# Graph attention with residual and layer norm: four steps of the loop moved between iterations, seventeen tiles of rows fetched one by one, 8.1 instead of 8.25 pick blocks an iteration

## The chip, the cores and the metric

The kernel runs on one core of one Trainium2 chip. The metric is the device time of one execution in microseconds (us), from its start to its end on the chip; times shown as "median" are over several runs. A core has five engines that run side by side: TensorE (PE in the profile, its weight loads PEld), VectorE (DVE), ScalarE (ACT), GpSimd (POOL) and SyncE (SP), which only issues transfers.

## What is computed

There are 6250 nodes with 64 features and 206,250 edges, sorted by destination. Each edge has 64 features of its own. With H = 4 heads of D = 16:

```python
Qh = (x @ Wq.T + bq).reshape(n, H, D)
Kh = (x @ Wk.T + bk).reshape(n, H, D)
Vh = (x @ Wv.T + bv).reshape(n, H, D)
Ee = (edge_attr @ We.T + be).reshape(-1, H, D)
score = (Kh[src] * Qh[dst] * (1.0 / np.sqrt(D)) * Ee).sum(-1)
score = jnp.exp(jnp.clip(score, -5.0, 5.0))
msg = Vh[src] * score[..., None]
wV = jax.ops.segment_sum(msg, dst, num_segments=n)
out = layernorm(x + wV.reshape(n, H * D))
```

The sources are random, so the rows of k and v have to be fetched by index for each edge. The destinations are sorted, so queries and sums lie in narrow windows of nodes.

## The kernel before

A tile is 128 edges; there are 1612 tiles. A group (the loop's `g`) is eight tiles, 202 groups; two groups make a step, and the sums over destinations are made once a step. A prologue of some 100 us makes tables in DRAM: `kv_tab` with a row of k and v (512 bytes) for each node, `q3_tab` with q in three bf16 parts. Then one long loop, written out by hand, goes over the groups. The order of the instructions on each engine is the order of the program; engines wait for each other through semaphores. A PSUM tile's bank is used by one instruction after another: two users of one bank wait for each other in program order even where they touch different columns. The tile `room` has two banks. Both hold edge values (`ee`); the first also holds the sums (`pa`, `sum_`) and the second the weights. The tile `qe` has a bank for each of two groups; `qq` is one bank.

For group g the steps are, with the engine and the profile's line:

- `edges(g)`, PE, L691 `room<-et,we_sb`: eight f32 matmuls make the edge values, transposed (features by edges), from the loaded `et`.
- `biased(g)`, ACT, L706 `eb<-room,be_col`: adds the bias.
- `queries(g)`, PE, L691 `qq<-to,qw`: two matmuls of a window of q with one-hot rows. The one-hot rows are made on ACT by `onehot_rows` (L247) and `onehot_rows_rest` (L253) from loaded keys `kb`.
- `terms(g)`, DVE, L721 `term<-eb,qq`: product of the two.
- `turn(g)`, PE, L727 `qe<-ident,term`: four transposes, back to edges by features.
- `products(g)`, DVE, L745 and L748: product with k, and the sum over each head.
- `weigh(g)`, ACT, L754 and L756: clip and exponential; the weights lie in `room`.
- `message(g)`, DVE, L768 `qe<-room,kv`: weights times v, into `qe`.
- `keep(g, 0)`, `take(g, 0)`, `keep(g, 1)`, `take(g, 1)`, ACT L782 and DVE L787: split the message into three bf16 parts (`msg`); keep rounds, take subtracts.
- `sums(s)`, PE, L691 `room<-msg,of`: 16 matmuls a step with a one-hot of destinations (`onehot_edges`, DVE, L737), into `room`.
- `add(s)`, DVE, L822 and L828: adds a step's sums to the node rows. It runs in the odd iterations, the sums in the even ones.

The rows of k and v come in three ways. The first five groups are computed in the prologue. Most tiles are gathered by GpSimd, one indirect transfer of 128 rows a tile (`gather`, L264). The others are "picked" on PE: `hots` (DVE, L651) makes a one-hot block of sources, and `picks` multiplies it with the node features `parts`, three matmuls of 128 by 512 a block (L691 `pick<-hot,parts`). 25 blocks pick the sources' features for one set of four tiles; `picked` (DVE, L673), `picked_kv` (PE, L691 `pick<-w,x`, with `bkv_p`) and `place_kv` (ACT, L686) make k and v of them. How many blocks an iteration does is set by `first_unit`, now 33/4 = 8.25; 63 sets are made in all.

In iteration g the order before is:

- PE: edges(g+3); the set's `picked_kv`, where one is due; all picks; turn(g+1); queries(g+2); in even iterations sums.
- DVE: products(g); hots; message(g); hots; take(g,0); in odd iterations add; where due, picked; in odd iterations onehot_edges; take(g,1); terms(g+2); normalising of finished rows.
- ACT: weigh(g); biased(g+3); onehot_rows(g+4); keep(g,0); where due, place_kv; onehot_rows_rest(g+4); keep(g,1).
- SP: transfers of `et` (every second iteration), source rows, `qw` and `kb` (every second), in this order.
- POOL: the gathers for four steps on, each tied to a PE instruction (`where`, `behind`) so that they are spread over the iteration.

Of the kernel before, what the change touches and what calls it, by code (L numbers as in the profile page):

```python
# [8 lines left out]
F32 = mybir.dt.float32  # L9
BF16 = mybir.dt.bfloat16  # L10
I32 = mybir.dt.int32
U8 = mybir.dt.uint8
# [4 lines left out]
P = 128  # L17
# [38 lines left out]
def tiles_of(g):  # L56
    return min(G, T - g * G)
# [19 lines left out]
def first_unit(g):  # L77

    return (g - LEAD) * 33 // 4


def when(k):

    return max(g for g in range(LEAD + 4 * k // 33 + 2) if first_unit(g) <= k)
# [17 lines left out]
def is_picked(g, j):  # L102

    return g in ALL_PICKED and j >= tiles_of(g) - 2

# [25 lines left out]
def tile_gnn(ctx: ExitStack, tc: tile.TileContext, x, x_blocks, by_rows, xT, wT, bias, beT, weT, eT, src, src_rows, dst,  # L131
             dst_rows, out):
# [10 lines left out]
    key_tab = dram.tile([NR2, 2 * G * P], U8, name="key_tab")  # L143
    kv_v = kv_tab.rearrange("(p b) c -> p b c", p=P)
# [4 lines left out]
    kvs = [consts.tile([P, 2 * G, 2 * C], F32, name=f"kv{i}") for i in range(KVB)]  # L149

# [117 lines left out]
    def lots(s):  # L268

        some = []  # L270
        for g in groups_of(s):
            js = [j for j in range(tiles_of(g)) if not is_picked(g, j)]
            some += [(g, js[:len(js) // 2]), (g, js[len(js) // 2:])]
        return some
# [17 lines left out]
    with tc.tile_pool(name="nodes", bufs=1) as nodes, \  # L292
# [161 lines left out]
        def rest_of_q():  # L454
            q, two = late.pop(0)
            nc.scalar.activation(q3[:, two, 1], q, AF.Copy)
            nc.vector.tensor_sub(q3[:, two, 2], q, q3[:, two, 1])

        for i in range(NB // CB):
            bs = slice(i * CB, (i + 1) * CB)  # L460
            kv_sb = chunks.tile([P, CB, 2 * C], F32, name="kv_sb")
            for b in range(0, CB, 2):
# [34 lines left out]
                if place == (4, 4):  # L497
                    masks()
                pair = (i * CB + b) // 2
# [14 lines left out]
            if i == 2:  # L514
                nc.sync.dma_start(x_nodes[1], by_rows[:, 30 * C:])
                nc.sync.dma_start(dst_i[:, :KEYS], dst[:, :KEYS])
        rest_of_q()
# [84 lines left out]
    with tc.If(rv == 0) as branch:  # L602

        with tc.tile_pool(name="work", bufs=2) as work, \
# [78 lines left out]
            def place_kv(m):  # L683
                for i, g in enumerate(PICKED[m]):
                    n = tiles_of(g)
                    nc.scalar.activation(kv_of(g)[:, n - 2:n, :], rooms_of(m)[:, 2 * i:2 * i + 2], AF.Copy)  # L686

# [186 lines left out]
            for g in range(2):  # L874
                edges(g)
                biased(g)
                queries(g)
                terms(g)
            turn(0)
            edges(2)  # L880
            biased(2)
            for mc in pieces(0):
                hots(*mc)
            for g in range(NG + 1):
# [37 lines left out]
                if parted:  # L922
                    take(g, 0)
# [20 lines left out]
                if parted:  # L944
                    keep(g, 1)
# [210 lines left out]
```

## Time and profile before

| | |
|---|---|
| median of 3 runs | 2070.77 us (2070.09 to 2071.17) |
| the profiled execution | 2091.55 us, of which the span of its instructions is 2089.7 |
| clock granted to TensorE, mean | 0.946 |
| busy: PE, DVE, POOL, ACT | 82%, 75%, 62%, 48% |
| memory traffic | 97 GB/s |

The profile is of one execution, and that one is some 21 us longer than the median of the runs. Busy times are shares of the span. A row of the groups reads: line, engine, operation, output tile and input tiles, shape, count, then busy time in us and the mean of one in ns, then the engine's idle time just before these instructions and what ended most of it. In a timeline row the first two numbers are start and duration in us, and the bracket gives the idle time before it and its releaser.

### The profile page before, as it was taken

What the parts mean: (1) busy time and instruction counts of PE and PEld (TensorE: products, weight loads), DVE (VectorE), ACT (ScalarE), POOL (GpSimd) and SP (SyncE); (2) the same over time, 40 slices, a digit from 0 to 9 for tenths busy, and PEclk for the clock granted to TensorE, in tenths of its full rate; (3) what the DMA queues carried; (4) which work ended last, traced back from release to release, by engine and by line L of the source; (5) the groups of instructions that cost most, each with busy time, mean ns of one, the idle gap of its engine ahead of it and who ended that gap; (6) DMA issues with size and microseconds to landing.
All of it is one profiled execution on the core that took longest, in us unless ns stands there. A gap on an engine that the chain in (4) does not pass through costs nothing.

```text
span 2089.7 us, 29080 instructions
## 1 busy us (share of the span) xinstructions
PE 1715.4 (82%) x9720; PEld 881.7 (42%) x9907; DVE 1563.1 (75%) x2484; ACT 995.5 (48%) x1712; POOL 1287.9 (62%) x1370
## 2 busy tenths in 40 slices
PE   6488798888888888888878888888888888878864
PEld 6244344444444444444434444444444443444432
DVE  5377777777777787777777778777877777778775
ACT  3454454445444455445444454444444544445553
POOL 6566666666666666666666666666666666666552
PEclk9789999999999999999999999999999999999975
DMA  6534333333333333333333333333333333333320
GB/s 174 191 92 117 89 99 100 84 101 101 81 102 85 102 97 86 102 92 102 100 82 100 96 93 102 83 99 102 82 111 90 98 101 82 101 87 95 95 81 24
DMA packets 115175, 203.87 MB, mean 98 GB/s; under 512 B 55427, under 2 KB 56175, under 8 KB 114901
## 3 DMA queue, kind: packets, MB, share of 16 engines
q1 hardware_dynamic: 71058, 112.94, 18.2%
q0 software_dynamic: 43520, 87.91, 16.5%
q8 instruction: 80, 1.31, 0.3%
q10 hardware_dynamic: 436, 1.04, 0.2%
q14 instruction: 81, 0.66, 0.1%
HBM read 194.18 MB, written 7.59 MB: 97 GB/s over the span
## 4 chain that ended last, share of the span: by engine, by line
PE 60%; DVE 14%; issue 11%; ACT 10%; another core or an unknown queue 2%; POOL 1%; DMA 1%; DVEq 0%; POOLq 0%; ACTq 0%; SPq 0%
PE pick L691 44%; PE room L691 12%; DVE hot L651 4%; ACT eb L706 3%; DVE qe L768 3%; DVE qe L787 2%; PE qe L727 2%; PE qq L691 1%; ACT room L756 1%; ACT to L253 1%; ACT to L247 1%; PE ps L467 1%; ACT msg L782 1%; POOL kv L264 1%
## 5 line engine op out<-in xcount | busy, mean ns | idle before, releaser
L264 POOL DMA_INDIRECT kv<-kv_tab,src_i x1320 | 1248.4, 946 | 747.1 <-issue 295.2
L691 PE MATMUL pick<-hot,parts 128*128 128x512 bf16 x4538 | 1110.1, 389 | 100.3 <-issue 88.0
L691 PEld LDWEIGHTS <-parts 128*128 128x128 bf16 x4725 | 455.2, 100 | 724.9 <-issue 270.6
L651 DVE TENSOR_TENSOR hot<-from,still 128x2560 bf16<-128x2560 bf16 (+4 forms) x411 | 469.5, 1149 | 0.0
L754 ACT ACTIVATE score<-score,five_p 128x32 f32<-128x32 f32 x202 | 64.9, 321 | 756.0 <-DVE score L748 419.8
L768 DVE SCALAR_TENSOR_TENSOR qe<-room,kv 128x512 f32<-128x512 f32 x200 | 139.9, 699 | 273.4 <-ACT eb L706 243.3
L691 PE MATMUL room<-et,we_sb 64*64 64x256 f32 (+1 forms) x1616 | 151.8, 428 | 141.3 <-DVE qe L787 33.0
L782 ACT ACTIVATE msg<-qe 128x512 bf16<-128x512 f32 x400 | 236.9, 592 | 7.0 <-DVE qe L787 4.3
L253 ACT ACTIVATE to<-to,one_p 126x1024 bf16<-126x1024 bf16 x198 | 227.3, 1148 | 0.0
L691 PE MATMUL room<-msg,of 128*128 128x192 bf16 x1592 | 159.5, 254 | 81.0 <-issue 26.9
L247 ACT ACTIVATE to<-kb,minus_row 126x1024 bf16<-126x1024 uint8 x198 | 224.8, 1135 | 0.0
L721 DVE TENSOR_TENSOR term<-eb,qq 128x512 f32<-128x512 f32 x202 | 137.1, 679 | 115.1 <-PE pick L691 35.3
L787 DVE TENSOR_TENSOR msg<-qe,msg 128x512 bf16<-128x512 f32 x200 | 137.0, 685 | 65.0 <-issue 28.0
L691 PEld LDWEIGHTS <-of 128*128 128x128 bf16 x1600 | 136.5, 101 | 107.8 <-issue 79.4
L756 ACT ACTIVATE room<-score,five_p 128x32 f32<-128x32 f32 x202 | 58.8, 291 | 232.4 <-PE pick L691 180.0
L706 ACT ACTIVATE eb<-room,be_col 128x512 f32<-128x512 f32 x202 | 138.6, 686 | 25.6 <-remote 15.9
L787 DVE TENSOR_TENSOR qe<-qe,msg 128x512 f32<-128x512 f32 x200 | 139.3, 696 | 6.9 <-ACT msg L782 3.6
L748 DVE TENSOR_REDUCE score<-prod 128x32 f32<-128x512 f32 x202 | 138.3, 684 | 7.0
L745 DVE TENSOR_TENSOR prod<-kv,qe 128x512 f32<-128x512 f32 x202 | 137.2, 679 | 5.3 <-issue 2.7
L727 PE MATMUL qe<-ident,term 128*128 128x128 f32 x806 | 126.0, 280 | 5.3 <-DVE term L721 4.9
L691 PEld LDWEIGHTS room<-et,we_sb 64*64 64x64 f32 x1616 | 49.1, 138 | 191.8 <-issue 125.9
L727 PEld LDWEIGHTS qe<-ident,term 128*128 128x128 f32 x806 | 102.7, 144 | 49.0 <-DVE term L721 9.6
(139 smaller groups left out, 972.5 us busy)
## 6 DMA issues: line engine op xcount, KB each, us to landing
et<-in_eT SPq DMA_DIRECT2D x100, 512.0 KB
kb<-key_tab SPq DMA_DIRECT2D x101, 252.0 KB
kv<-kv_tab,src_i POOLq DMA_INDIRECT x1320
srcs<-in_src_rows SPq DMA_DIRECT2D x63, 256.0 KB
qw<-q_tab SPq DMA_DIRECT2D x202, 15.8 KB
kv_tab<-kv_sb SPq DMA_DIRECT2D x4, 640.0 KB
q_tab<-q SPq DMA_DIRECT2D x5, 480.0 KB
y<-in_x_blocks SPq DMA_DIRECT2D x2, 512.0 KB
```

What stands on the lines that cost most here:

```text
L247: nc.scalar.activation(TO[g][:, :n, :], KB.pop(g)[:, :n * P].rearrange("p (j e) -> p j e", j=n), AF.Square, bias=minus_row3[:3 * W])
L253: nc.scalar.activation(TO[g][:, :n, :], TO[g][:, :n, :], AF.Relu, bias=one_p[:3 * W], scale=-1.0)
L264: return nc.gpsimd.indirect_dma_start(out=kv_of(g)[:, j, :], out_offset=None, in_=kv_tab[:, :], in_offset=bass.IndirectOffsetOnAxis(ap=src ...
L651: nc.vector.tensor_tensor(HOT[k][:, :hi - lo].rearrange("p b (a c) -> p b a c", c=2), pairs(FROM[m])[:, None].to_broadcast(shape), block2[ ...
L691: mark.append(nc.tensor.matmul(*aps, **kw))
L706: nc.scalar.activation(EB[g][:, :n].rearrange("p (i r) e -> p r i e", r=2), ee[:, :, :n // 2], AF.Identity, bias=be_col)
L727: nc.tensor.transpose(qe[g % 2][:, k:k + half + 1:half, :], TERM[g][:, k, :], ident)
L745: nc.vector.tensor_mul(prod[:, :n, :], kv_of(g)[:, :n, :C], qe[g % 2][:, :n, :])
L748: nc.vector.tensor_reduce(score, prod[:, :n, :].rearrange("p g (h d) -> p g h d", h=H), axis=AX.X, op=OP.add)
L768: nc.vector.scalar_tensor_tensor(to.rearrange("p g (h d) -> p g h d", h=H), WEIGHT.pop(g)[:, :, :, None].to_broadcast([P, n, H, D]), LEAST ...
L782: nc.scalar.activation(part, left, AF.Copy)
L787: nc.vector.tensor_sub(left if i == 0 else part_of(g, 2)[1], left, part)
```

## The change

Three things are changed.

The number of pick blocks an iteration becomes 81/10 = 8.1; with it the number of sets becomes 62, and the sets' places move.

Seventeen tiles (the first tile of groups 13, 24, ... 189) are neither gathered nor picked. Their 128 rows are fetched by SyncE with one transfer for each row: the row's byte offset is read into a register from `single_i`, and 512 bytes are copied from `kv_tab` into a tile `single`. Twelve rows are fetched in an iteration, over eleven iterations a tile; two iterations after the last, ScalarE copies the tile to its place (`place_single`).

Four steps move. In iteration g the order becomes:

- PE: `picked_kv` where due; four blocks of picks; edges(g+3); turn(g+1); queries(g+2); the other picks; in even iterations sums.
- DVE: products(g); take(g-1,1); terms(g+1); hots; message(g); hots; add; picked; onehot_edges; take(g,0); normalising.
- ACT: keep(g-1,1); weigh(g); biased(g+2); place_single; onehot_rows(g+4); keep(g,0); place_kv; onehot_rows_rest(g+4).
- SP: as before, and then the twelve rows.

The diff, without the plumbing of the new input:

```diff
 def first_unit(g):
-    return (g - LEAD) * 33 // 4
+    return (g - LEAD) * 81 // 10
...
+EACH = 12
+SPAN = -(-P // EACH)
+SINGLE = list(range(SPAN + 2, NG - 3, SPAN))
...
+            def fetch_singles(g):
+                i, lo = g // SPAN, g % SPAN * EACH
+                if i >= len(SINGLE):
+                    return
+                if lo == 0:
+                    SINGLES[i] = work.tile([P, 2 * C], F32, name="single")
+                hi = min(lo + EACH, P)
+                _, vs = nc.values_load_multi_w_load_instructions(
+                    single_i[i:i + 1, lo:hi], engines=[mybir.EngineType.SP], min_val=0,
+                    max_val=(NR - 1) * 2 * C * 4, skip_runtime_bounds_check_because="rows of the sources")
+                for p, v in zip(range(lo, hi), vs):
+                    nc.sync.dma_start(SINGLES[i][p:p + 1, :].bitcast(U8), kv_bytes[:, bass.ds(v, 2 * C * 4)])
+
+            def place_single(g):
+                if g in SINGLE:
+                    nc.scalar.activation(kv_of(g)[:, 0, :], SINGLES.pop(SINGLE.index(g)), AF.Copy)
...
+                fetch_singles(g)
+                former = before and step_of[g - 1] < WHOLE
                 fetch_blocks(g)
                 where.append(mark[-1])
-                if g + 3 < NG:
-                    edges(g + 3)
+                if former:
+                    keep(g - 1, 1)
                 if now:
                     products(g)
+                if former:
+                    take(g - 1, 1)
+                if g + 1 < NG:
+                    terms(g + 1)
+                if now:
                     weigh(g)
-                if g + 3 < NG:
-                    biased(g + 3)
+                if g + 2 < NG:
+                    biased(g + 2)
                 for mc in ahead[:1]:
                     hots(*mc)
                 if now:
                     message(g)
+                place_single(g + 1)
...
-                if parted:
-                    take(g, 0)
                 for s in done:
                     add(s)
...
-                for some in by_two(todo):
+                two = by_two(todo)
+                for some in two[:2]:
                     picks(some)
                     where.append(mark[-1])
+                if g + 3 < NG:
+                    edges(g + 3)
                 if g + 1 < NG:
                     turn(g + 1)
                 if g + 2 < NG:
                     queries(g + 2)
+                for some in two[2:]:
+                    picks(some)
+                    where.append(mark[-1])
...
-                if parted:
-                    keep(g, 1)
...
                 if parted:
-                    take(g, 1)
-                if g + 2 < NG:
-                    terms(g + 2)
+                    take(g, 0)
```

More of the change, by code (lines that the diff above doesn't have):

```diff
@@ L77, in first_unit @@
 def first_unit(g):
-    return (g - LEAD) * 33 // 4
+    return (g - LEAD) * 81 // 10
 def when(k):
-    return max(g for g in range(LEAD + 4 * k // 33 + 2) if first_unit(g) <= k)
+    return max(g for g in range(LEAD + 10 * k // 81 + 2) if first_unit(g) <= k)
 LAST = max(m for m in range(1, NG) if when(UNITS * m - 1) + 8 < NG)
@@ L104, in is_picked, with is_single @@
     return g in ALL_PICKED and j >= tiles_of(g) - 2
+EACH = 12
+SPAN = -(-P // EACH)
+SINGLE = list(range(SPAN + 2, NG - 3, SPAN))
+assert SINGLE[0] >= 10
+def is_single(g, j):
+    return g in SINGLE and j == 0
 BLOCKS = (RING, 24, 4), (24, 40, READY[0] + 4), (40, BIG + 1, READY[0] + 6)
@@ L149, in tile_gnn @@
     kvs = [consts.tile([P, 2 * G, 2 * C], F32, name=f"kv{i}") for i in range(KVB)]
+    single_i = consts.tile([len(SINGLE), P], I32, name="single_i")
     def kv_of(g):
@@ L271, in lots @@
         for g in groups_of(s):
-            js = [j for j in range(tiles_of(g)) if not is_picked(g, j)]
+            js = [j for j in range(tiles_of(g)) if not is_picked(g, j) and not is_single(g, j)]
             some += [(g, js[:len(js) // 2]), (g, js[len(js) // 2:])]
@@ L873, in tile_gnn @@
             fetch_edges(2)
[L874 to L878, printed above, removed]
+            edges(0)
+            biased(0)
+            queries(0)
+            terms(0)
             turn(0)
+            edges(1)
+            biased(1)
+            queries(1)
             edges(2)
-            biased(2)
             for mc in pieces(0):
```

9 lines of the change are left out of this document (7 added, 2 removed).

## The prediction

> **What bounds the kernel now.** I read the page first (busy shares and clock), then the groups of lines, then a table by stretches, then the timeline of three iterations.
>
> ```profile
> span 2089.7 us, 29080 instructions
> PE 1715.4 (82%) x9720; PEld 881.7 (42%) x9907; DVE 1563.1 (75%) x2484; ACT 995.5 (48%) x1712; POOL 1287.9 (62%) x1370
> ...
> L264 POOL DMA_INDIRECT kv<-kv_tab,src_i x1320 | 1248.4, 946 | 747.1 <-issue 295.2
> L691 PE MATMUL pick<-hot,parts 128*128 128x512 bf16 x4538 | 1110.1, 389 | 100.3 <-issue 88.0
> L651 DVE TENSOR_TENSOR hot<-from,still 128x2560 bf16<-128x2560 bf16 (+4 forms) x411 | 469.5, 1149 | 0.0
> L691 PE MATMUL room<-et,we_sb 64*64 64x256 f32 (+1 forms) x1616 | 151.8, 428 | 141.3 <-DVE qe L787 33.0
> L691 PE MATMUL room<-msg,of 128*128 128x192 bf16 x1592 | 159.5, 254 | 81.0 <-issue 26.9
> ```
>
> PE is the busiest engine and two thirds of its work are picks. They overlap, so one costs 1110.1 us / 4538 = 245 ns, not its mean of 389. PE is idle for 2089.7 - 1715.4 = 374 us. Of that, 141.3 us end at the edge-value matmuls, 81.0 at the sums and 100.3 at the picks; the last are almost all "issue", which no reordering of data touches. So 222 us of PE's idle time stand before the two steps whose surroundings change. That is the gain's upper end.
>
> ```profile
> 300.00:1900.00 1600.00, 1359.53 (x7835) 682.22 (x7990) 1231.56 (x1871) 772.04 (x1295) 1011.79 (x1071) 0.97 0.35 95
> 926.10:933.16 7.06, 7.01 (x38) 3.19 (x39) 6.95 (x12) 4.65 (x8) 3.95 (x5) 0.94 0.15 39
> 1004.10:1012.55 8.45, 7.28 (x39) 3.24 (x39) 6.20 (x11) 4.39 (x7) 5.59 (x7) 0.92 0.19 45
> ...
> L768 DVE SCALAR_TENSOR_TENSOR qe<-room,kv 128x512 f32<-128x512 f32 x161 | 112.6, 699 | 212.9 <-ACT eb L706 191.1 <-issue 14.0 <-ACT room L756 5.2
> ```
>
> Columns of the first three: stretch, length, busy time of PE, PEld, DVE, ACT, POOL, then clock, DMA share and GB/s. The middle 1600 us hold 161 messages, so an iteration takes 1600 / 161 = 9.94 us. The iteration from 926.10 to 933.16 needs 7.06 with PE busy for 7.01 of it; the one from 1004.10 needs 8.45, and PE stands for 1.17. VectorE's message waits 212.9 us in this window, mostly for ScalarE's eb.
>
> ```profile
> 1001.90 2.27 PE L691 MATMUL room<-msg,of 128*128 128x192 bf16 x14 [1.17 <-issue]
> ...
> 1004.10 1.13 PE L691 MATMUL room<-et,we_sb 64*64 64x256 f32 x8
> ...
> 1008.16 0.29 ACT L756 ACTIVATE room<-score,five_p 128x32 f32<-128x32 f32 x1 [2.17 <-PE pick L691]
> ...
> 1008.48 0.69 ACT L706 ACTIVATE eb<-room,be_col 128x512 f32<-128x512 f32 x1
> ...
> 1009.20 0.70 DVE L768 SCALAR_TENSOR_TENSOR qe<-room,kv 128x512 f32<-128x512 f32 x1 [2.18 <-ACT eb L706]
> ...
> 1009.81 1.21 DVE L651 TENSOR_TENSOR hot<-from,still 128x2048 bf16<-128x2048 bf16 x1
> ...
> 1010.49 0.60 PE L727 MATMUL qe<-ident,term 128*128 128x128 f32 x4
> ...
> 1010.94 0.69 DVE L787 TENSOR_TENSOR qe<-qe,msg 128x512 f32<-128x512 f32 x1
> ...
> 1011.54 0.36 DVE L822 TENSOR_REDUCE room<-room 128x64 f32<-128x192 f32 x1
> ...
> 1011.93 0.28 DVE L828 SCALAR_TENSOR_TENSOR y<-room,above,y 128x64 f32<-128x64 f32 x1
> ...
> 1012.13 0.27 DVE L828 SCALAR_TENSOR_TENSOR y<-room,below,y 128x64 f32<-128x64 f32 x1
> ...
> 1012.55 0.66 PE L691 MATMUL room<-et,we_sb 64*64 64x256 f32 x8 [1.12 <-ACT to L253]
> ```
>
> This is the present ring. The tile `room` holds the edge values, the weights and the sums, and its users go one after the other. Edge values end at 1004.10 + 1.13 = 1005.23, but ScalarE's Exp, which writes `room`, starts only at 1008.16: PE's signal comes 2.93 us late, while picks run. Then biased (eb), message, hot, subtraction and add follow, and the next edge values start at 1012.55, right after the add (1012.40), PE having stood for 1.12.
>
> **The change, part by part.** *Ring cut.* Exp of iteration g now needs the edge values made in the middle of iteration g-1, with some 12 picks (12 x 0.245 = 2.9 us) and more behind them; the late signal above is about covered. The edge values stand behind four blocks (12 picks, 2.9 us) instead of at PE's start, so the add has 2.9 us more to finish. In half of the iterations (odd ones) the add still stands in front of them. I take half of 141.3: -70 us. Bounds: -141 if every wait goes, 0 if they come back at the new place (above 0: second rival).
>
> *Subtractions.* keep(g,1) and take(g,1) go behind the next products; sums(g+1) of PE still stand half an iteration behind that. Of the 81.0 us, 26.9 are "issue" and stay as they are; of the other 54 I take 20, since the subtraction now lies closer to its reader. Bounds 0 and -54. On ScalarE, keep waits at the head of the iteration and Exp is queued behind it, but Exp waits for the products anyway. On VectorE, take and terms now lie between products and message, where message idled for 212.9 us: the work hides in that wait, and ScalarE's Exp and biased (0.29 + 0.69) in the work.
>
> *Picks.* 81/10 instead of 33/4 blocks an iteration leaves 62 sets of 25 blocks instead of 63. 25 x 3 = 75 picks x 245 ns = 18.4 us off PE; one set's matmuls of k and v:
>
> ```profile
> L691 PE MATMUL pick<-w,x 128*128 128x128 f32 x504 | 79.3, 299 | 4.5 <-issue 4.3
> L686 ACT ACTIVATE kv<-pick 128x256 f32<-128x256 f32 x126 | 41.4, 387 | 6.2 <-PE pick L691 3.9 <-PE qq L691 1.6 <-PE qe L727 0.6
> ```
>
> 8 x 79.3 / 504 = 1.3 us. Together -20 us, as PE is on the path nearly everywhere (0 if another engine is). VectorE saves 469.5 x 25 / 1575 = 7.5 us beside it. The set's 4 tiles return to gathers and 17 tiles leave them: 13 gathers fewer, 12 us, hidden, since GpSimd idles for 747.1 us.
>
> *Single rows.* 17 x 128 = 2176 transfers of one row, 12 an iteration, by SyncE. Placing a tile costs ScalarE at most the 387 ns of L686, 17 times, 7 us: ScalarE is 48% busy, so nothing; the conversions behind it start that much later and are wanted some iterations on. The one product of offsets on VectorE is at the start: below 1 us. Issuing:
>
> ```profile
> 977.46 0.25 SPq L222 DMA_DIRECT2D qw<-q_tab  x1
> 977.81 0.34 SPq L241 DMA_DIRECT2D kb<-key_tab  x1
> 978.33 0.33 SPq L222 DMA_DIRECT2D qw<-q_tab  x1
> ...
> 995.39 0.36 SPq L208 DMA_DIRECT2D et<-in_eT  x1
> ...
> 999.01 0.00 SPq L222 DMA_DIRECT2D qw<-q_tab  x1
> ...
> L216 SPq TENSOR_LOAD <-base x26: 97/707/1484, 67.6 to 1973.4; - x26
> SPq L208 <- PE pick L691: 1007.9, 62, 22.3
> ```
>
> An issue with its address registers takes 978.33 - 977.81 = 0.52 us in one round, and (999.01 - 995.39) / 5 = 0.72 us in another. 12 x 0.52 + 0.71 (registers) + 1.0 (a generous half of a two-iteration round of et, kb, qw, srcs) = 8.0 us of an iteration. SyncE now waits for over 1007.9 us, so this fits; queued behind the rows are the next qw, kb and et, which are wanted two or three iterations on. I take 0. Bounds: 0 and the third rival's price.
>
> The Trainium skill, "DMA: Bandwidth & Descriptors", section "Issuing engine by pattern", gives indirect access to GpSimd and simple loads to SyncE, which speaks against this part. The trace shows no single-row transfer, so only SyncE's issue rows bear on it, and they leave room.
>
> *Clock.* The window's 0.97 means 0.03 x 1600 = 48 us of lost clock; the iteration after the 1.17 us stall at 1001.90 had 0.92. Shorter stalls may give part of it back. I count 0 and keep 48 for the range.
>
> The Trainium skill, "TensorE: Matmul & The Clock Gate", section "Why this matters for your kernels", fears only idle gaps above about 3 us. By that rule the 48 would stay lost; the row with 0.92 after 1.17 us speaks against it.
>
> **Sum.** -70 - 20 - 20 = -110 on the profiled execution's 2091.6 us (2089.7 span and 1.9 around it): 1981.6. The median of the runs is 2070.8, 20.8 lower; taken off likewise, 1960.8, say 1960.
>
> **The rivals.** *A, the forecast:* PE's waits halve; 1960.
>
> *B, slower: a new ring through the transposes.* Now message(g) -> edge values(g+3) -> turn(g+1) -> products(g+1) -> message(g+1) closes within one iteration, where before there was an iteration of slack. Its parts:
>
> ```profile
> 1013.45 0.68 DVE L787 TENSOR_TENSOR msg<-qe,msg 128x512 bf16<-128x512 f32 x1
> 1014.05 0.67 DVE L721 TENSOR_TENSOR term<-eb,qq 128x512 f32<-128x512 f32 x1
> 1014.64 0.68 DVE L745 TENSOR_TENSOR prod<-kv,qe 128x512 f32<-128x512 f32 x1
> 1015.36 0.69 DVE L748 TENSOR_REDUCE score<-prod 128x32 f32<-128x512 f32 x1
> 1015.96 1.48 DVE L651 TENSOR_TENSOR hot<-from,still 128x2560 bf16<-128x2560 bf16 x1
> ...
> 1016.98 0.29 ACT L756 ACTIVATE room<-score,five_p 128x32 f32<-128x32 f32 x1 [0.58 <-PE pick L691]
> ...
> 926.10 1.06 PE L691 MATMUL room<-et,we_sb 64*64 64x256 f32 x8
> ...
> 928.77 0.29 ACT L756 ACTIVATE room<-score,five_p 128x32 f32<-128x32 f32 x1
> ```
>
> PE 0.66 + 0.60, VectorE 0.68 + 0.69 + 0.68 + 0.67 + 1.48 + 0.70: 6.16 us plus PE's late signal. With an add before the edge values, also 1.21 + 0.36 + 0.28 + 0.27: 8.28. Mean 7.22 plus the lag. It decides once the lag exceeds 9.94 - 7.22 = 2.7 us. The lag was 2.93 above, 1016.98 - 1013.21 = 3.77 in the next iteration, and at most 928.77 - 927.16 = 1.61 in the quick one. With the mean of the first two, 3.35, an iteration takes 10.57: 0.63 x 191 iterations with picks = +120 us; 2190. For it: those two lags. Against: they were seen with a whole iteration's picks, 8.25 x 3 or some 25, in one run behind the edge values; now transposes, queries and waits of their own follow at once, and runs of picks are half as long. I expect 1 to 2 us.
>
> *C, slower: SyncE becomes the bound.* At the second round's pace 12 x 0.72 + 0.71 + 1.8 = 11.2 us an iteration, +1.2 us x 187 iterations = +225; about 2295. At 0.52 it is 8.0 and costs nothing; it decides from (9.94 - 1.7) / 12 = 0.69 us a row. Against: the pace of 0.52 is seen where nothing was in the way.
>
> *D, the waits only change place.* VectorE (75%) and the adds end last again, and only the 20 us of removed matmuls are gained: 2050.
>
> **How the numbers follow.** A 0.50, B 0.24, C 0.09, D 0.17. The likeliest is A, so 1960. A's own range: 1856 (141 + 54 + 20 us gained) to 2020 (50 gained). The range for all cases leaves out A's last tenth below and C with B's worst lags above: 1875 to 2200. A measurement of this kernel tells 0.2%, 4 us, from no change. Faster: A 0.50, D 0.12, C 0.01 = 0.63. Same: D 0.04, B 0.01 = 0.05. Slower: B 0.23, C 0.08, D 0.01 = 0.32.
>
> **What would show it.** Right: idle before the edge-value matmuls falls from 141.3 to about 70 and before the sums to about 60; message's idle time before it nearly vanishes; picks number 75 fewer; an iteration takes about 9.4 us; SyncE still waits for PE at its et issue. Wrong by B: VectorE's products (L745), now without a wait, wait for PE's qe, and the edge values wait for message longer than before. Wrong by C: SyncE's waits vanish and conversions or queries wait for DMA. Wrong by D: the same idle sums at new lines, total down by 20.

## The result, and the profile after

The changed kernel takes 2173.47 us (median of 4 runs, 2163.61 to 2179.02) against 2070.97 for the kernel before, measured beside it: 1.049 times as long, with an interval of 1.045 to 1.053. The profiled execution has a span of 2173.9 us, against 2089.7.

These lines are from the page of the changed kernel. The line numbers have moved: L726 is the old L691, L780 the old L745, L791 the old L756, L803 the old L768.

```profile
span 2173.9 us, 33489 instructions
PE 1769.1 (81%) x9823; PEld 878.9 (40%) x9823; DVE 1538.8 (71%) x2481; ACT 1021.2 (47%) x1726; POOL 1275.9 (59%) x1357
...
L726 PE MATMUL pick<-hot,parts 128*128 128x512 bf16 x4650 | 1132.3, 398 | 2.8 <-issue 2.6
...
L726 PE MATMUL room<-et,we_sb 64*64 64x256 f32 (+1 forms) x1616 | 154.6, 455 | 342.8 <-issue 215.5
L780 DVE TENSOR_TENSOR prod<-kv,qe 128x512 f32<-128x512 f32 x202 | 138.3, 685 | 303.8 <-PE pick L726 149.6
...
L726 PE MATMUL room<-msg,of 128*128 128x192 bf16 x1592 | 153.0, 249 | 6.3 <-issue 5.5
```

Read the idle column of PE's three large groups. Before, edge values, picks and sums had 141.3 + 100.3 + 81.0 = 322.6 us ahead of them. Now they have 342.8 + 2.8 + 6.3 = 351.9. The waits ahead of the picks and of the sums are nearly gone, and about as much has come up ahead of the edge values. The new sign is in the fourth group: VectorE's products, which hardly waited before (4.3 us in the middle 1600 us, row further down), now wait for 303.8 us over the span.

PE is busy for 53.7 us more, although it has 75 picks and one set's matmuls of k and v less to do. Its idle time has grown by only 30.5 us (2173.9 - 1769.1 = 404.8 against 374.3). Some 10 us of this are records: the trace before holds 4538 of its 4725 picks, and the idle gaps under 0.15 us ahead of picks, which the missing ones leave, add up to 11.9 us there and to 0.2 now. For the rest the stretches of the changed kernel say why. Columns as before: length, busy time of PE, PEld, DVE, ACT, POOL, then clock.

```profile
300.00:1900.00 1600.00, 1343.30 (x7575) 650.40 (x7573) 1157.19 (x1787) 756.59 (x1247) 962.20 (x1018) 0.92 0.33 91
1018.59:1022.60 4.01, 4.01 (x18) 1.66 (x19) 3.70 (x7) 1.48 (x3) 0.94 (x1) 0.50 0.14 38
1022.60:1030.00 7.40, 7.40 (x41) 3.22 (x40) 5.81 (x9) 4.75 (x7) 4.71 (x5) 0.96 0.20 41
```

The clock of the middle 1600 us fell from 0.97 to 0.92. The second row begins where PE had stood for 6.33 us (the edge values at 1018.59 below): it then ran at 0.50 all through the 4.01 us of this row. The Trainium skill, "TensorE: Matmul & The Clock Gate", section "Why this matters for your kernels", gives gaps above about 3 us as what sends PE back to half speed; this stall agrees with it. Shorter gaps can go with it too: the trace before has 23 stretches at 0.50 in its middle 1600 us, and around 18 of them (9 us before to 3.5 us after their start) PE has no gap above 3 us, as the prediction read from its stall of 1.17 us.

The timeline of the changed kernel shows one odd iteration, the one with the longest of the waits in question.

```profile
1003.95 0.69 DVE L780 TENSOR_TENSOR prod<-kv,qe 128x512 f32<-128x512 f32 x1 [1.64 <-PE qe L762]
...
1005.88 9.09 SPq L717 DMA_DIRECT2D single<-kv_tab  x12
...
1006.78 1.48 PE L726 MATMUL room<-msg,of 128*128 128x192 bf16 x16
...
1014.84 0.29 ACT L791 ACTIVATE room<-score,five_p 128x32 f32<-128x32 f32 x1 [9.12 <-remote]
...
1015.88 0.70 DVE L803 SCALAR_TENSOR_TENSOR qe<-room,kv 128x512 f32<-128x512 f32 x1 [7.94 <-ACT eb L741]
...
1018.21 0.28 DVE L863 SCALAR_TENSOR_TENSOR y<-room,below,y 128x64 f32<-128x64 f32 x1
...
1018.59 1.13 PE L726 MATMUL room<-et,we_sb 64*64 64x256 f32 x8 [6.33 <-issue]
1019.65 1.11 PE L762 MATMUL qe<-ident,term 128*128 128x128 f32 x4
...
1020.80 0.69 DVE L780 TENSOR_TENSOR prod<-kv,qe 128x512 f32<-128x512 f32 x1 [0.24 <-PE qe L762]
```

The sums end at 1006.78 + 1.48 = 1008.26. Exp, which writes the same tile `room`, starts at 1014.84, 6.58 us later; the mean of such waits in the middle 1600 us is 2.55. The bias copy, message and add follow, then the edge values, the transposes behind them, and the next products. PE worked off picks until 1012.26 and then stood for 6.33 us. In the same stretch SyncE's twelve row issues took 9.09 us, the longest of all.

### The profile page after: what moved, and what is told of

Its sections match the earlier page's. It is cut to its first block, busy times and chain, and to the rows that moved or that the text cites. A ratio compares the mean times of both kernels' runs of the same rounds, so it can differ in the third digit from the quotient of the medians.

```text
span 2173.9 us, 33489 instructions
## 1 busy us (share of the span) xinstructions
PE 1769.1 (81%) x9823; PEld 878.9 (40%) x9823; DVE 1538.8 (71%) x2481; ACT 1021.2 (47%) x1726; POOL 1275.9 (59%) x1357
## 4 chain that ended last, share of the span: by engine, by line
PE 69%; issue 10%; DVE 9%; ACT 7%; another core or an unknown queue 4%; DMA 1%; SPq 0%; POOL 0%; ACTq 0%; DVEq 0%; POOLq 0%
PE pick L726 45%; PE room L726 12%; PE qe L762 6%; PE qq L726 4%; ACT to L260 2%; ACT eb L741 2%; DVE hot L666 2%; DVE prod L780 1%; DVE score L783 1%; PE ps L480 1%; DVE qe L803 1%; ACT room L791 1%; DVE msg L822 1%; ACT msg L817 1%
## 5 line engine op out<-in xcount | busy, mean ns | idle before, releaser
L726 PE MATMUL pick<-hot,parts 128*128 128x512 bf16 x4650 | 1132.3, 398 | 2.8 <-issue 2.6
L726 PEld LDWEIGHTS <-parts 128*128 128x128 bf16 x4650 | 455.9, 102 | 592.9 <-issue 163.1
L666 DVE TENSOR_TENSOR hot<-from,still 128x2560 bf16<-128x2560 bf16 (+4 forms) x409 | 463.2, 1139 | 3.5 <-issue 1.7
L726 PE MATMUL room<-et,we_sb 64*64 64x256 f32 (+1 forms) x1616 | 154.6, 455 | 342.8 <-issue 215.5
L780 DVE TENSOR_TENSOR prod<-kv,qe 128x512 f32<-128x512 f32 x202 | 138.3, 685 | 303.8 <-PE pick L726 149.6
L803 DVE SCALAR_TENSOR_TENSOR qe<-room,kv 128x512 f32<-128x512 f32 x200 | 139.0, 695 | 249.1 <-ACT eb L741 130.0
L726 PEld LDWEIGHTS room<-et,we_sb 64*64 64x64 f32 x1616 | 48.9, 145 | 433.2 <-issue 267.3
L791 ACT ACTIVATE room<-score,five_p 128x32 f32<-128x32 f32 x202 | 58.8, 291 | 341.9 <-PE pick L726 238.3
L762 PE MATMUL qe<-ident,term 128*128 128x128 f32 x806 | 160.8, 332 | 13.9 <-issue 10.6
L726 PE MATMUL room<-msg,of 128*128 128x192 bf16 x1592 | 153.0, 249 | 6.3 <-issue 5.5
L726 PEld LDWEIGHTS <-of 128*128 128x128 bf16 x1600 | 137.6, 99 | 31.0 <-issue 6.8
L756 DVE TENSOR_TENSOR term<-eb,qq 128x512 f32<-128x512 f32 x202 | 136.5, 676 | 14.0 <-DMA kv<-kv_tab,src_i 11.1
```

Source lines behind the costliest of these rows:

```text
L666: nc.vector.tensor_tensor(HOT[k][:, :hi - lo].rearrange("p b (a c) -> p b a c", c=2), pairs(FROM[m])[:, None].to_broadcast(shape), block2[ ...
L726: mark.append(nc.tensor.matmul(*aps, **kw))
L762: nc.tensor.transpose(qe[g % 2][:, k:k + half + 1:half, :], TERM[g][:, k, :], ident)
L780: nc.vector.tensor_mul(prod[:, :n, :], kv_of(g)[:, :n, :C], qe[g % 2][:, :n, :])
L803: nc.vector.scalar_tensor_tensor(to.rearrange("p g (h d) -> p g h d", h=H), WEIGHT.pop(g)[:, :, :, None].to_broadcast([P, n, H, D]), LEAST ...
```

## The experiments

Theories named in the expectations: **S**, in odd iterations Exp stands behind the sums in `room`; **R**, SyncE's row issues cost time; **T**, rival B's ring, message - edge values - transposes - products; **U**, any wait for PE costs alike; **V** and **W**, the moved subtractions (and terms) cost; **L**, PE's signals are late on some chips only; **G**, GpSimd's gathers are a bound.

The runs fell on several chips, and the kernel before takes 2071 to 2094 us on some of them and 1730 on others, so each kernel is given as a ratio to before on its own chip. "First kind" is a chip like that of the result, "quicker kind" one with 1730.

### On the first kind (before 2094.38 us): the parts one by one

**Without the single rows** (all else as changed).

```diff
 def is_single(g, j):
-    return g in SINGLE and j == 0
+    return False
...
-                fetch_singles(g)
...
-                place_single(g + 1)
```

> The changed kernel without the single-row transfers: the seventeen tiles are gathered by GpSimd again, nothing is fetched or placed by SyncE's rows; the new order and 8.1 blocks stay. Theory S (the new order puts the Exp of odd iterations behind the sums in the tile room, and PE's late signal then decides): about as slow as the changed kernel, 2140 to 2180 us, with 200 us or more of idle time before the edge-value matmuls. Theory R (SyncE's 2176 issues delay PE's signals): at or below the kernel before, 1960 to 2070 us, and PE's signal reaches the Exp within 3 us.

2147.44 us, 1.0257 (1.0227 to 1.0287). About half of the 1.049 measured on the other chip stays without any row by SyncE: R alone is out.

**The single rows alone**: the loop of the kernel before, with 8.1 blocks and with `fetch_singles(g)` and `place_single(g + 1)` in it (the first lines of the edit against the changed kernel).

```diff
-            edges(0)
-            biased(0)
...
+            for g in range(2):
+                edges(g)
+                biased(g)
...
```

> The order of before with 8.1 blocks and the seventeen tiles' rows by SyncE: only the moves of the steps are undone. Theory S: 2040 to 2060 us, the 20 us of removed matmuls below the kernel before. Theory R: 2090 to 2170 us, since the late signals also sit in the old ring from the edge values to the Exp.

2112.31 us, 1.0091 (1.0068 to 1.0114).

**8.1 blocks alone**: the same without the rows.

> The order of before, no single rows, only 8.1 instead of 8.25 blocks: 17 more gathers than in the changed kernel. Both theories: 2045 to 2065 us by the 20 us of removed matmuls; up to 2075 if PE is not on the path there.

2096.88 us, 1.0017 (1.0005 to 1.003). Both theories missed: 20 us less work for PE gained nothing. So the rows alone cost 0.7%, and the new order without them 2.4%.

**The sums early**: the changed kernel with the sums ahead of the remaining picks.

```diff
                 if g + 2 < NG:
                     queries(g + 2)
+                if g - 1 in ends and now:
+                    sums(ends[g - 1])
                 for some in two[2:]:
                     picks(some)
                     where.append(mark[-1])
                 where.append(mark[-1])
-                if g - 1 in ends and now:
-                    sums(ends[g - 1])
```

> The changed kernel with the sums put right behind the queries, ahead of the second half of the picks, so that 12 to 15 more picks (about 3 us of PE) lie between the sums and the edge values that wait for Exp, message and add behind them. Theory S: 1950 to 2070 us, idle before the edge values falls by half or more. Theory R: 2130 to 2180 us. Theory T (the ring through the transposes that the prediction priced): no change either, 2150 to 2180 us.

2183.97 us, 1.0433 (1.0406 to 1.0459). The groups of its middle 1600 us:

```profile
L780 DVE TENSOR_TENSOR prod<-kv,qe 128x512 f32<-128x512 f32 x153 | 105.2, 688 | 392.4 <-PE pick L726 282.3 <-remote 43.7 <-PE qq L726 25.4
L791 ACT ACTIVATE room<-score,five_p 128x32 f32<-128x32 f32 x154 | 44.8, 291 | 72.7 <-PE pick L726 55.1 <-PE room L726 8.3 <-remote 5.4
```

and the same groups of the changed kernel:

```profile
L780 DVE TENSOR_TENSOR prod<-kv,qe 128x512 f32<-128x512 f32 x153 | 105.0, 686 | 226.6 <-PE pick L726 109.0 <-PE room L726 41.9 <-PE qq L726 38.3
L791 ACT ACTIVATE room<-score,five_p 128x32 f32<-128x32 f32 x154 | 44.8, 291 | 279.4 <-PE pick L726 205.5 <-remote 49.4 <-PE room L726 21.6
L803 DVE SCALAR_TENSOR_TENSOR qe<-room,kv 128x512 f32<-128x512 f32 x154 | 107.0, 695 | 199.0 <-ACT eb L741 108.7 <-ACT room L791 42.6 <-issue 30.5
```

and before the change:

```profile
L745 DVE TENSOR_TENSOR prod<-kv,qe 128x512 f32<-128x512 f32 x160 | 108.9, 681 | 4.3 <-issue 2.4 <-DMA kv<-kv_tab,src_i 0.2
L756 ACT ACTIVATE room<-score,five_p 128x32 f32<-128x32 f32 x161 | 46.9, 291 | 191.1 <-PE pick L691 156.7 <-remote 25.0 <-PE qq L691 4.5
```

With the sums early Exp waits 72.7 us instead of 279.4, and products wait 165.8 us more. The changed kernel ran on another chip of this kind; without the rows, on this chip, the two waits were 166.0 and 309.9. S had the wait right but not what it decides: another wait took its place, and it is the one ahead of products, as T has it.

### On the quicker kind: cutting T's ring

**Weights in a tile of their own** (without rows): the edge values no longer wait for message.

```diff
-                WEIGHT[g] = weights[g % 3][:, :n]
+                WEIGHT[g] = work.tile([P, G, H], F32, name="weight", bufs=3)[:, :n]
```

> The changed kernel without the single rows, and Exp writes the weights into a tile of their own in SBUF instead of into room: the edge values no longer wait for message, and Exp no longer waits for the sums. Compare with the kernel without single rows (2147). Theory T, the ring message - edge values - turn - products is what the new order costs: the idle time ahead of products in the window 300 to 1900 falls from 310 us to under 150, and the time to 2060 to 2115. Rival U, it is the number of times an iteration in which VectorE or ScalarE waits for one of PE's late signals, whatever ring that belongs to: products' idle time stays above 250 and the time at 2130 to 2155. Rival V, the subtraction moved ahead of terms and message on VectorE is what costs: as U here.

1748.66 us against 1730.07: 1.0115 (1.0098 to 1.0132).

**The same in the order of before.**

> The order of before, 8.1 blocks an iteration, no single rows, and the weights in a tile of their own in SBUF: Exp no longer waits for the edge values of the same iteration, message's writer and the edge values are uncoupled. Compare with 2097. If before is bound by the ring edge values - Exp - biased - message - edge values with PE's late signal in it, as the prediction read it: Exp's idle time falls from 224 us to under 60 and the time to 2030 to 2080. If the wait only changes place (U, and the prediction's D): 2085 to 2100, with the idle time ahead of message or terms grown.

1750.08 us: 1.0122 (1.0105 to 1.0139). Here Exp waited for only 5.0 us that could be freed, so this edit costs 1.2% by itself; the reason was not tested. In its trace a gather took 961 ns, against 948 in the kernel before on that kind. The first of the two is therefore only a hint for T.

**Transposes first** (without rows): one exchange in PE's order.

```diff
-                if g + 3 < NG:
-                    edges(g + 3)
                 if g + 1 < NG:
                     turn(g + 1)
+                if g + 3 < NG:
+                    edges(g + 3)
```

> The changed kernel without the single rows, with the transposes one step ahead of the edge values on PE instead of behind them; nothing else. The transposes then no longer stand behind PE's wait for message. Compare with 2147. T: products' idle time falls from 310 us to under 150 and the time to 2060 to 2115. U and V: products' idle time above 250, 2130 to 2155.

1730.61 us: 1.0005 (0.9995 to 1.0014). The same kernel without the exchange takes 1775.32 on another chip of this kind (below).

**Subtractions alone**, in the order of before (the edit against it).

```diff
+                if former:
+                    keep(g - 1, 1)
                 if now:
                     products(g)
+                if former:
+                    take(g - 1, 1)
...
-                if parted:
-                    take(g, 0)
...
-                if parted:
-                    keep(g, 1)
...
                 if parted:
-                    take(g, 1)
+                    take(g, 0)
```

> The order of before, 8.1 blocks an iteration, no single rows, and of the change's moves only the two subtractions and the copy of the second part (to the end of the iteration and to the head of the next). Compare with the kernel with 8.1 blocks alone (2097). T: edge values, terms and transposes stay where they were, so 2080 to 2105; the term of the prediction was -20, which would be 2075 to 2080. V: 2130 to 2160. U: 2090 to 2105.

1730.65 us: 1.0006 (0.9996 to 1.0015): nothing on this kind. On the first kind V was not tried. Products' idle time from 300 to 1600 us did rise, from 4.2 us in before to 78.6, but the time did not.

Next, on one chip of this kind: before once more for its trace (no code changed), the changed kernel, it without the rows, and the whole change with the transposes first.

> The kernel before again, for its trace on the same chip as the three beside it. Theory L, the signals from PE are late on some chips and not on others: where before takes about 1730 us, Exp's idle time ahead of it and the time from the end of the edge values to Exp's start are a fraction of those in the first trace (191 us in the window 300 to 1900, mean 5.1 us), and GpSimd's gathers follow one another every 1.25 us; where it takes about 2080 us, the first trace returns. Rival, the slower chip has a lower clock alone: then PE's own matmuls are longer by the 20% and waits are as they were.

> The changed kernel again, beside the next two. Theory T, the ring message - edge values - turn - products, priced by PE's signal: at a before of about 2080 us, 1.04 to 1.055; at about 1730 us, where signals are prompt, 0.99 to 1.01. Theory S, Exp behind the sums in room, which holds on any chip: 1.02 or more at 1730 too. R, SyncE's issues cost time by themselves: over the kernel without rows by 0.01 or more on either chip.

> The changed kernel without the single rows (those tiles by GpSimd again). At a before of about 2080 us: 1.022 to 1.03, as measured. At 1730: T 0.995 to 1.01; where GpSimd's gathers are the bound there (290 gathers of every 300 at 1.25 us), the rows' 17 tiles are worth 21 us, and this is slower than the changed kernel by 0.005 to 0.012.

> The whole changed kernel, single rows and all, with the transposes one step ahead of the edge values on PE. T: the transposes no longer stand behind PE's wait for message; at a before of about 2080 us it takes back 25 us or more of the changed kernel's time (ratio under 1.035) and products' idle time falls from 227 us to under 100; at 1730 us it is within 0.005 of the changed kernel or faster. U, S: within 0.008 of the changed kernel on either chip.

Before took 1729.54 us (one run, the others 1729.06). Changed: 1775.5, 1.0272 (1.0254 to 1.0289). Without rows: 1775.32, 1.0266 (1.0249 to 1.0283). Transposes first, with rows: **1710.03, 0.989 (0.9874 to 0.9907)**, faster than both kernels. T had expected the changed kernel at 0.99 to 1.01 here, so it was wrong that the ring needs late signals; S's 1.02 or more was met, but S, like U, saw nothing to gain from the exchange. T did: two steps of PE in the other order are worth 65 us. The groups from 300 to 1600 us of before on this chip:

```profile
L264 POOL DMA_INDIRECT kv<-kv_tab,src_i x1039 | 984.5, 948 | 316.8 <-DMA kv<-kv_tab,src_i 115.9 <-issue 102.8 <-PE pick L691 55.2
L691 PE MATMUL room<-et,we_sb 64*64 64x256 f32 x1272 | 105.4, 400 | 30.3 <-DVE y L828 21.3 <-ACT msg L782 7.6 <-DVE acc L828 0.7
L756 ACT ACTIVATE room<-score,five_p 128x32 f32<-128x32 f32 x158 | 46.0, 291 | 5.0
```

of the changed kernel:

```profile
L277 POOL DMA_INDIRECT kv<-kv_tab,src_i x1020 | 967.4, 948 | 334.0 <-issue 182.1 <-PE pick L726 85.4 <-PE room L726 20.0
L780 DVE TENSOR_TENSOR prod<-kv,qe 128x512 f32<-128x512 f32 x153 | 104.4, 683 | 27.6 <-PE qe L762 18.3 <-DMA kv<-kv_tab,src_i 5.6 <-issue 0.6
L726 PE MATMUL room<-et,we_sb 64*64 64x256 f32 x1224 | 102.0, 402 | 69.3 <-ACT msg L817 37.8 <-ACT to L266 16.2 <-DVE qe L803 8.3
L791 ACT ACTIVATE room<-score,five_p 128x32 f32<-128x32 f32 x154 | 44.8, 291 | 197.6 <-PE room L726 195.2
```

and with the transposes first:

```profile
L277 POOL DMA_INDIRECT kv<-kv_tab,src_i x1038 | 984.3, 948 | 316.8 <-issue 110.2 <-DMA kv<-kv_tab,src_i 106.8 <-PE pick L726 49.4
L780 DVE TENSOR_TENSOR prod<-kv,qe 128x512 f32<-128x512 f32 x159 | 108.1, 680 | 4.8 <-DMA kv<-kv_tab,src_i 1.9 <-issue 0.6
L726 PE MATMUL room<-et,we_sb 64*64 64x256 f32 x1272 | 105.4, 400 | 48.3 <-issue 27.6 <-DVE qe L803 10.6 <-ACT to L266 9.3
L791 ACT ACTIVATE room<-score,five_p 128x32 f32<-128x32 f32 x159 | 46.3, 291 | 182.7 <-PE room L726 177.6 <-issue 2.6
```

In before, Exp has 5.0 us of idle time in these 1300 us, against 191.1 in the middle 1600 us on the first kind, as L has it. Its edge values wait 30.3 us; 69.3 in the changed kernel. With the transposes first, products' wait for PE is gone. Exp's wait for the sums stays (182.7), and the kernel is faster all the same.

GpSimd's row suggests what the rows are for. In before, 1039 gathers fill the 1300 us, one in every 1.25 us; by their starts in the trace none follows the one ahead in under 1.24 us, and none in over 1.5: GpSimd is full. 17 tiles less are 17 x 1.25 = 21 us; with the transposes first, rows against no rows is 1710.03 against 1730.61, 20.6 us less (two chips, before 1.0 us apart). In the changed order GpSimd has gaps (1020 gathers, 20 of them over 1.5 us behind the one ahead), and the rows gain nothing.

### What the moves do singly, and the first kind again

**PE's moves alone**: the order of before, with edge values, transposes and queries behind the first four blocks; subtractions and terms as before; no rows (the edit against the kernel before).

```diff
-                if g + 3 < NG:
-                    edges(g + 3)
                 if now:
                     products(g)
                     weigh(g)
-                if g + 3 < NG:
-                    biased(g + 3)
+                if g + 2 < NG:
+                    biased(g + 2)
...
-                for some in by_two(todo):
+                two = by_two(todo)
+                for some in two[:2]:
                     picks(some)
                     where.append(mark[-1])
+                if g + 3 < NG:
+                    edges(g + 3)
                 if g + 1 < NG:
                     turn(g + 1)
                 if g + 2 < NG:
                     queries(g + 2)
+                for some in two[2:]:
+                    picks(some)
+                    where.append(mark[-1])
```

> The order of before, 8.1 blocks an iteration, no single rows; of the change's moves only the PE ones: edge values, transposes and queries behind the first four blocks, with the biased copy one iteration later as it must be. Subtractions and terms stay as before. T, the ring message - edge values - turn - products is made by this move alone: ratio 1.015 to 1.04 at a before of about 1730 us, 1.02 to 1.04 at about 2080 us. Rival W, it takes terms and subtractions between products and message too: 0.995 to 1.01 on either.

1863.5 us against 1729.85: 1.078 (1.0762 to 1.0798), worse than either side expected. From 300 to 1600 us:

```profile
L780 DVE TENSOR_TENSOR prod<-kv,qe 128x512 f32<-128x512 f32 x147 | 100.1, 681 | 3.9 <-issue 1.5 <-DMA kv<-kv_tab,src_i 0.6
L726 PE MATMUL room<-et,we_sb 64*64 64x256 f32 x1180 | 98.3, 401 | 104.4 <-ACT msg L817 94.1 <-ACT to L266 5.3 <-DVE qe L803 5.0
```

Products don't wait here; PE does. Its row names ScalarE's `msg` (keep), which stands behind message; in the iteration whose edge values start at 1007.71 us that ends at 1007.61, and so does the add. So the loop that costs here does not close through products, as T has it. By the order of the steps it can close through PE alone (edge values, picks, sums, Exp, message, add, edge values); this was read from the order and not tested, and the three moved steps were not tried apart. Moving subtractions and terms as well takes two thirds of the loss back: 1.078 to the 1.0266 of the changed kernel without rows (another chip of this kind).

**Rows alone** in the order of before, on this kind (the second kernel of the first section).

> The order of before, 8.1 blocks an iteration, 17 tiles' rows by SyncE. At a before of about 2080 us 1.0068 to 1.0114, as measured. At about 1730 us: theory G, GpSimd's gathers are the bound of the old order there (one every 1.25 us, 13 fewer net and 17 moved, 30 x 1.25 = 16 to 21 us): 0.988 to 0.993. Rival R, SyncE's issues cost time: 1.00 to 1.01.

1726.33 us: 0.9986 (0.9976 to 0.9996). Neither side: a gain of 3.5 us, a fifth of the 13 x 1.25 = 16 us that 13 gathers fewer should free. So a full GpSimd is not the whole bound of before on this kind; what else holds it was not found.

**Transposes first and sums early** (the edit against the kernel with the transposes first), and the transposes first once more.

```diff
                 if g + 2 < NG:
                     queries(g + 2)
+                if g - 1 in ends and now:
+                    sums(ends[g - 1])
                 for some in two[2:]:
...
-                if g - 1 in ends and now:
-                    sums(ends[g - 1])
```

> The whole changed kernel with the transposes ahead of the edge values, and the sums directly behind the queries instead of behind the remaining picks. If Exp behind the sums (2.2 us in every odd iteration, S) is next on the path: faster than the kernel with the transposes first by 0.005 or more, and Exp's wait under 0.5 us. If PE is full by then (1252 of 1300 us busy): within 0.003 of it.

> The whole changed kernel with the transposes ahead of the edge values, a second time. At a before of about 1730 us 0.987 to 0.991, as measured. At about 2080 us, where the changed kernel stood at 1.045 to 1.053: T, and the ring is the whole cause there too: under 1.01. T with late signals and rows beside it: 1.01 to 1.035. The ring is not the cause there: 1.04 or more.

1706.52 us, 0.9864 (0.9848 to 0.9881), and 1710.51 us, 0.9886 (0.9867 to 0.9904): the sums early are unclear here, the intervals overlap.

The last two runs, these two kernels again, fell on the first kind (before 2071.32).

> The whole changed kernel with the transposes ahead of the edge values, a third time, with more rounds. At a before of about 1730 us 0.987 to 0.991. At about 2080 us, where the changed kernel stood at 1.045 to 1.053: T alone, under 1.01; T beside late signals and the rows, 1.01 to 1.035; the ring is not the cause there, 1.04 or more.

> The same with the sums directly behind the queries, a second time with more rounds. At a before of about 1730 us 0.002 to 0.003 below the kernel beside it, since its Exp no longer waits. At about 2080 us, where a signal that is waited for costs more: 0.01 or more below it, if Exp behind the sums is a cause of its own; within 0.004, if the wait goes elsewhere, as it did with the sums early alone.

2119.07 us, 1.0217 (1.019 to 1.0244), and 2094.63 us, 1.0119 (1.0101 to 1.0138). The groups of the first from 300 to 1900 us:

```profile
L726 PE MATMUL room<-et,we_sb 64*64 64x256 f32 x1261 | 115.3, 436 | 217.0 <-issue 159.0 <-ACT to L266 14.4 <-DVE qe L803 11.7
L780 DVE TENSOR_TENSOR prod<-kv,qe 128x512 f32<-128x512 f32 x157 | 107.0, 682 | 102.4 <-PE pick L726 48.1 <-remote 17.4 <-PE qe L762 13.8
L791 ACT ACTIVATE room<-score,five_p 128x32 f32<-128x32 f32 x157 | 45.7, 291 | 388.3 <-PE pick L726 208.7 <-PE room L726 62.4 <-PE qe L762 60.2
```

and of the second:

```profile
L726 PE MATMUL room<-et,we_sb 64*64 64x256 f32 x1272 | 111.9, 422 | 119.3 <-issue 70.9 <-DVE qe L803 20.7 <-DVE hot L666 16.3
L780 DVE TENSOR_TENSOR prod<-kv,qe 128x512 f32<-128x512 f32 x160 | 108.8, 680 | 124.5 <-PE pick L726 76.5 <-remote 26.0 <-DMA kv<-kv_tab,src_i 11.3
L791 ACT ACTIVATE room<-score,five_p 128x32 f32<-128x32 f32 x159 | 46.3, 291 | 291.4 <-PE pick L726 181.7 <-remote 105.7 <-PE room L726 2.3
```

On this kind the 4.9 points of the result (on another chip) come apart so: 2.7 go when the transposes no longer stand behind the edge values (products' wait 226.6 to 102.4 us, though Exp's rose from 279.4 to 388.3), 1.0 more when the sums come early (the edge values' wait 217.0 to 119.3): Exp behind the sums is a second cause, as S said. The last 1.2 are left. In the order of before the rows cost 0.7 and the blocks 0.2; out of the changed kernel the rows took 2.3 with them (1.049 to 1.0257, on two chips), so the parts overlap. This order without rows was not tried on this kind. Neither version beats before on this kind; on the quicker kind both do.

## Why the prediction was wrong

The forecast, A, was 1960 us and faster. It went as B had it: B's 2190 us and 10.57 us an iteration stand against 2173.47 and 1600 / 154 = 10.39 (154 messages in the middle window). The sign that B named, products waiting for PE, was there, and the exchange that takes the transposes out of B's ring took back over half (on another chip). So the mechanism was on the list, at 0.24. That B's time came out so near is in part luck: it put one lag of 3.35 us into the loop, where the runs show two smaller ones, and it had no wait of Exp for the sums. On the quicker kind, where lags were 0.1 to 0.3 us, its sum of 7.22 us plus the lag lies under before's 1300 / 158 = 8.23 us an iteration and would cost nothing; 2.7% were measured.

- **Ring cut (-70), the step that failed.** It said that Exp needs edge values from the iteration before, so that the late signal is covered. That is so in even iterations. In odd ones the sums now come between the edge values and Exp, and they use `room` too. They lie in its first bank and the weights in its second, and Exp waited all the same: on the quicker kind 76 of its 77 waits ended 0.10 us after the sums. So users of the tile, and not only of a bank, wait for each other here. Read from the starts and ends in the trace, Exp's idle time after its input was 0.07 us in even and 3.60 in odd iterations on average; before it had been 0.81 and 1.63. The wait ahead of the edge values rose by 201.5 us over the span instead of falling by 70. Message's idle time, in which the moved work was to hide, stayed (212.9 to 199.0 us in the middle 1600).
- **B's lag, 1 to 2 us.** Where products waited they started 1.79 us after the transposes' end on average, within that. But where Exp waited it started 2.55 us after the sums' end (a tenth of the cases above 4.4), and by the order of the steps that lag stands in the same loop; B counted one of two. The argument that shorter runs of picks make signals prompt had no row behind it.
- **Subtractions (-20).** Nothing by themselves in the order of before (1.0006, on the quicker kind only). The waits before sums and picks did nearly vanish, but turned into one ahead of the edge values. Beside PE's moves, subtractions and terms together were worth 5 points there.
- **Picks (-20).** 1.0017 alone: no gain. "PE is on the path nearly everywhere" was wrong: with 75 picks fewer PE's idle time was 2095.0 - 1699.5 = 395.5 us, against 374.3 before (another chip), so PE waited longer with less work. Nor was it right that no reordering touches the picks' idle time marked "issue": it went from 100.3 to 2.8 us. (The count of picks did not fall in the pages, 4538 and 4650, since the first trace lacks 187.)
- **Single rows (0).** 0.7% in the order of before, on the first kind; in the new order 2.3 points, on two chips, and nothing on the quicker kind. How they cost is open: where they waited, Exp started 2.55 us after the sums' end with the rows and 1.26 without, but products 1.79 us after the transposes with and 2.63 without. Rival C is not what happened: in the list of waits SyncE's `et` issue still waits for PE's edge values for 184.5 us, and for its picks for 88.5.
- **Clock (0).** It fell to 0.92, which is 0.05 x 1600 = 80 us of full speed. It is not the whole cause: where the clock stayed at 1.00 (the quicker kind, both kernels), the change still cost 2.7%.

## What to carry to other kernels

When a step is moved on an engine, list every reader and writer of its tile in the new program order, for even and odd iterations apart: here the sums slipped between the edge values and Exp, and the transposes behind a wait. Put steps that wait for nothing late (the transposes) ahead of the one that waits, not behind it. A lag that was seen twice in the trace is the price to use until a row shows a smaller one, and it can belong to the chip: 2.55 us here, 0.10 there. A kernel that gains on one kind of chip can lose on the other (0.989 and 1.022).

## What the runs showed of the hardware that was not expected

The same kernel takes 1730 us on some chips and 2071 to 2094 on others. VectorE's and ScalarE's instructions last as long on both (products 682 and 681 ns, Exp 291 ns), and picks nearly so (380 and 389 ns). The difference is in what follows: where Exp of the changed kernel waited for the sums, it started 0.10 us after their end on the quicker kind and 2.55 us on the first. The trace's record of the semaphores says where that time lies. On the first kind PE's semaphore is counted up late, and Exp starts 0.08 us after the count (median) on both kinds; in the iteration shown above the count came at 1014.75. Signals between VectorE and ScalarE are prompt on the first kind too: in the changed kernel clip started 0.04 us after VectorE's score in each of 150 waits, and message 0.03 us after ScalarE's bias copy in each of 62.

On the first kind there are stretches over 0.45 us in which no instruction of any engine starts: 163 of them between 300 and 1500 us in before, 104 us together; on the quicker kind 6, 3.7 us. They are not what slows the changed kernel, which has fewer (79, 47 us). What holds PE's signals back was not found. The ends of matmuls in the trace are modelled, so PE itself may have been later than shown. Nor is it excluded that the recording plays a part: on the first kind the trace of the changed kernel holds 1256 of the 2249 counts of VectorE's semaphore, on the quicker kind 2238.

SyncE's row issues are slower on the first kind too. From 300 to 1600 us of the changed kernel twelve rows with their address registers took 5.7 us on average there and 4.2 on the quicker kind. With the transposes first, on the quicker kind, this is a common case:

```profile
1000.02 3.82 SPq L717 DMA_DIRECT2D single<-kv_tab  x12
```

That is 0.32 us a row. The Trainium skill, "DMA: Bandwidth & Descriptors", section "Issuing engine by pattern", gives indirect access to GpSimd; where GpSimd was full, rows by SyncE were worth 20.6 us with the transposes first and 3.5 in the order of before, and where it had gaps, nothing or a loss.
